# The second layer norm of a fused cross-attention block, moved from ScalarE and GpSimd to VectorE

## The chip, the cores and the metric

The kernel runs on one core of a Trainium2 chip. The metric is the device time of one execution in microseconds. The profile is of one execution, taken by the hardware profiler; its times count from its first instruction. The core has five engines that work side by side, each through its own list of instructions: TensorE (PE; its weight loads are PEld), VectorE (DVE), ScalarE (ACT), GpSimd (POOL), and SyncE (SP), which here only issues DMAs.

## The reference

Everything is float32. For 128 sequences of 128 tokens with 256 features:

```python
q = (query @ Wq + bq).reshape(b, s, 16, 16).transpose(0, 2, 1, 3)
k = (key @ Wk + bk)...            # key and values are ctx_1024
v = (values @ Wv + bv)...
scores = einsum('bhqd,bhkd->bhqk', q, k) / 4
scores = where(j < i, scores, -1e30)
attn = softmax(scores); attn[:, :, 0, :] = 0
attn_out = (attn @ v) @ Wo + bo
x = layer_norm(query + attn_out, ln1_g, ln1_b)
ffn = relu(x @ W1 + b1) @ W2 + b2          # 256 -> 1024 -> 256
out = layer_norm(x + ffn, ln2_g, ln2_b)
```

where `layer_norm(x, g, b) = (x - mu) * rsqrt(var + 1e-5) * g + b` over the 256 features. The change concerns the last line.

## The kernel before

The 128 sequences are worked in 64 pairs; a tile such as `t2` holds one pair as 128 tokens x 2 x 256. The work is software-pipelined by hand: in step p the kernel does the scores and the softmax of pair p, the attention product of pair p-2, the hidden layer of pair p-3, the second matrix of the feed-forward net of pair p-4, and the second layer norm of pair p-5. The schedule is manual: the order of the calls in the source is the order in which each engine gets its instructions, and semaphores only make an engine wait. For pairs 9 to 60 the order is one table of names with lags (lines 1493 to 1513), looked up in `ops` (lines 1359 to 1492); the steps before and after are written out call by call (lines 1567 to 2333 and 2336 to 2915).

What the steps below touch, in the order of one step:

- `scores_both` (L486) writes the scores of a pair into PSUM banks 0 to 3 (second half of the queries) and 6, 7, 4, 5 (first half). `mask` (L511) on VectorE reads the latter; its first call of a step is the one of bank 4 (`low2`). The query products of the next pair (`Query.run`, L351) write bank 4 again, so they come after that mask.
- The softmax runs on ScalarE (L997). `reciprocal` (L566) on VectorE, `sums` (L557) on GpSimd and `turn` (L574, a transpose of 32x32 blocks on VectorE) follow, three times a step. `bring` (L608) moves the transposed blocks by DMA on SP's queue, in which the DMAs of the first norm (`leave_x1` L256, `fetch_x1` L262) stand as well.
- The hidden layer is made of seven products (Strassen's scheme, L1156), which VectorE adds up in `hT` (L1175 to L1187); ScalarE applies the relu in place (L1190), GpSimd forms the sums `hS` for the next stage (L1023 to L1029).
- The second matrix is seven products as well (S1 to S7, L1064); VectorE adds them into `t2` (L1088). S5 is `py<-wt,hS`.
- `Joint` (L1301) collects the statistics of two norms at once: bn_stats (L1313) and bn_aggr (L1318) on VectorE give mean and variance `mv`; `both_shifts` (L720) on GpSimd gives `sd`, the variance plus eps to the power -0.5, and `nb`, minus mean times `sd` (L717, L718, L723, L724).
- `norm2` (L783) then scales and shifts `t2` in place on ScalarE, one half of the pair at a time (`n2a`, `n2b`, L787). `finish` (L791) multiplies by `g2_r` and adds `be2_r` on GpSimd, over the whole pair at once (`fin1` L794, `fin2` L796). `g2_r` and `be2_r` are the two vectors of 256, repeated on all 128 partitions of SBUF. `store` (L815) sends `t2` out on SP's queue two steps later.
- GpSimd's other work of a step: `add_bo` (L274), the residual's scale and shift (L761, L765), the combinations for the seven products of the queries (L320 to L326) and of the hidden layer (L1110 to L1116).

In the table, `n2b` stands before `rcp0`, which is followed by the last sum into `t2` (`add5`) and the hidden adds; `n2a` stands after `Hadd3` and before `turn2`; `fin1` stands after `turn2`; `fin2`, with lag 2, stands among the `hS` sums two steps later.

Pairs 0, 1, 58 and 59 call `norm2` and `finish` directly, 60 to 62 use `norm2_apart` and `finish_apart`, and the last pair ends in `last_scale` (L1553) and `last_shift` (L1559), which are scalar_tensor_tensor instructions on VectorE with one operand in PSUM. Only one early pair normalizes on VectorE (L749, tensor_scalar on an SBUF tile, twice).

Of the kernel before, what the change touches and what calls it, by code (L numbers as in the profile page):

```python
# [11 lines left out]
ALU = mybir.AluOpType  # L12
# [8 lines left out]
def tile_cross_attention_block(  # L21
# [22 lines left out]
    nc = tc.nc  # L44
# [30 lines left out]
    states = {}  # L75
# [45 lines left out]
    def row(v, name, at=None):  # L121
        t = const.tile([P, v.shape[1]], F32, tag=name, name=name) if at is None else early[:, at : at + v.shape[1]]
        nc.sync.dma_start(t, v.to_broadcast([P, v.shape[1]]))
        return t
# [40 lines left out]
    g2_r = row(ln2_g, "g2_r")  # L165
    be2_r = row(ln2_b, "be2_r")
# [49 lines left out]
    def at_bank(i, name):  # L216
        return psum.tile([P, 512], F32, tag=f"b{i}", name=name)
# [519 lines left out]
    def norm1(p, parts=range(2)):  # L737

        st = states[p]
        x1 = st["x1"] = st["t1"]  # L740
        t1, mv, sd = x1, st["mv", 1], st["sd", 1]
        for s in parts:
            if p != 1:

                nc.scalar.activation(
                    x1[:, s], t1[:, s], AF.Identity, bias=st["nb", 1][:, s], scale=sd[:, s]
                )
                continue
            nc.vector.tensor_scalar(  # L749
                x1[:, s], t1[:, s], mv[:, s, 0:1], sd[:, s], ALU.subtract, ALU.mult  # L750
            )

    def residual1(p, engine=nc.gpsimd, parts=range(2)):

        st = states[p]
        if 0 in parts:
            if p < NP - 2:
                st["t2"] = ffn.tile([P, 2, D], F32, tag="t2", name=f"t2_{p}", bufs=4)
            else:
                st["t2"] = proj.tile([P, 2, D], F32, tag="xb", name=f"t2_{p}")  # L760
            engine.tensor_tensor(  # L761
                st["t2"], st["x1"], g1_r[:, None, :].to_broadcast([P, 2, D]), ALU.mult
            )
        if 1 in parts:
            engine.tensor_tensor(  # L765
                st["t2"], st["t2"], be1b_r[:, None, :].to_broadcast([P, 2, D]), ALU.add
            )
# [15 lines left out]
    def norm2(p, parts=range(2)):  # L783
        st = states[p]
        t2, sd, nb = st["t2"], st["sd", 2], st["nb", 2]
        for s in parts:
            nc.scalar.activation(  # L787
                t2[:, s], t2[:, s], AF.Identity, bias=nb[:, s], scale=sd[:, s]
            )

    def finish(p, parts=range(2)):  # L791
        t2 = states[p]["t2"]
        if 0 in parts:
            nc.gpsimd.tensor_tensor(t2, t2, g2_r[:, None, :].to_broadcast([P, 2, D]), ALU.mult)  # L794
        if 1 in parts:
            nc.gpsimd.tensor_tensor(t2, t2, be2_r[:, None, :].to_broadcast([P, 2, D]), ALU.add)  # L796

    def norm2_apart(p, at, parts=range(2)):

        st = states[p]  # L800
        t2, sd, nb = st["t2"], st["sd", 2], st["nb", 2]
        ps = once("pb", p, lambda: at_bank(at, f"pb_{p}").rearrange("p (s d) -> p s d", s=2))
        for s in parts:
            nc.scalar.activation(
                ps[:, s], t2[:, s], AF.Identity, bias=nb[:, s], scale=sd[:, s]
            )
# [8 lines left out]
    def store(p):  # L815
        nc.sync.dma_start(
            out[2 * p : 2 * p + 2].rearrange("b p d -> p b d"), states.pop(p)["t2"]
        )
# [212 lines left out]
    def once(kind, p, make):  # L1031
        st = states[p]
        if kind not in st:
            st[kind] = make()
        return st[kind]
# [180 lines left out]
    for which, first in (("c", c_first[:, 0:2]), ("x", tokens_of[0][:, 0:2])):  # L1216
        st = states[0]
# [113 lines left out]
    def second7(p):  # L1331
        return once("second", p - 4, lambda: Second(p - 4, 6))
# [25 lines left out]
    def step_tables():  # L1358
# [93 lines left out]
            "shifts": lambda p: joint(p).shifts(),  # L1452
            "n1a": lambda p: norm1(p - 2, (0,)),
            "n1b": lambda p: norm1(p - 2, (1,)),
            "n2a": lambda p: norm2(p - 5, (0,)),
            "n2b": lambda p: norm2(p - 5, (1,)),
            "add0": lambda p: second7(p).add(0),
            "add1": lambda p: second7(p).add(1),
            "add2": lambda p: second7(p).add(2),
# [18 lines left out]
            "bo": lambda p: add_bo(p - 1),  # L1478
            "x1g": lambda p: residual1(p - 3, nc.gpsimd, (0,)),
            "x1b": lambda p: residual1(p - 3, nc.gpsimd, (1,)),  # L1480
            "fin1": lambda p: finish(p - 5, (0,)),
            "fin2": lambda p: finish(p - 5, (1,)),
            "store": lambda p: store(p - 5),
            "tbx": lambda p: block_x1(p - 2),
            "x1out": lambda p: leave_x1(p - 2),
# [28 lines left out]
        return ops, order  # L1514

    ops, order = step_tables()

    def steps(first, last):
# [1305 lines left out]
    h62.relu(4)  # L2824
    both_shifts(*j60a)
    norm2_apart(60, 4, (0,))
    w61.add(4)
    norm2_apart(60, 4, (1,))
    w62 = Second(62, banks=(0, 7, 2))
    w62.run(2)  # L2830
# [56 lines left out]
    w62.add(5)  # L2887
    j62a = both_stats((), (62,))
    norm2_apart(61, 3, (1,))
    both_shifts(*j62a)  # L2890
    norm2_apart(61, 3, (0,))
# [59 lines left out]
```

## Time and profile before

| | |
|---|---|
| runs | 1477.25 and 1477.29 us, median 1477.27 us |
| profiled execution: span, first to last instruction | 1476.5 us |
| mean granted TensorE clock | 0.999 of full |
| one step of the steady stretch | 22.45 us |
| pairs normalized through the table's `n2a`, `n2b`, `fin1`, `fin2` | 56 of 64 (2 to 57) |

The profile's page gives the busy time of each engine as a sum and as a share of the span. The timeline has a row for each instruction (equal neighbours are merged, with their count): start and length in us, engine, line, operation, output tile <- input tiles, shapes. A wait in brackets is idle time of that engine just before the row, with the engine, tile and line that ended it. Instructions of one engine overlap a little, so the work that an instruction costs its engine is the distance from its start to the next one's start when nothing is waited for; this is called the hand-over below. Rows of groups give the total busy time and the mean in ns; rows of one line give least, median and greatest duration.

### The profile page before, as it was taken

The page shows a single profiled execution, that of the slowest core. Times are in us where ns is not written, and L with a number is a line of the kernel's source. Part 1 is how long each engine was busy: PE and PEld are TensorE (multiplying, and loading weights), DVE is VectorE, ACT ScalarE, POOL GpSimd, SP SyncE. Part 2 cuts the span into 40 slices and gives each one's busy share as a digit, 9 for nine tenths or more (in the row PEclk, how much of TensorE's full clock was granted, in tenths as well). Part 3 has the DMA queues.
Part 4 walks back from the last instruction along what each step waited for, and adds up shares of the span by engine and source line. Part 5 has one row for each costly group of instructions (what it writes and reads, how often), then busy time and mean ns, then how long its engine had stood idle before and what let it go on. Part 6 is the DMA issues. An engine that isn't in the chain of part 4 may idle for free.

```text
span 1476.5 us, 53972 instructions
## 1 busy us (share of the span) xinstructions
PE 1463.9 (99%) x19696; PEld 1377.8 (93%) x19696; DVE 1315.5 (89%) x2897; ACT 1323.0 (90%) x5279; POOL 1388.2 (94%) x1484
## 2 busy tenths in 40 slices
PE   9999999999999999999999999999999999999998
PEld 7788999999999999999999999999999999999998
DVE  7999899999998998998998999989989999999866
ACT  5758999999999999999999999999999999999863
POOL 7788999999999999999999999999999999999987
PEclk9999999999999999999999999999999999999999
DMA  8465566655656666666556566556565666664451
GB/s 203 96 141 127 133 146 139 147 138 136 156 141 138 141 146 139 148 144 145 138 135 154 139 142 141 144 135 157 141 139 136 146 141 150 136 152 122 116 162 58
DMA packets 417865, 206.22 MB, mean 140 GB/s; under 512 B 282434, under 2 KB 386114, under 8 KB 417602
## 3 DMA queue, kind: packets, MB, share of 16 engines
q1 hardware_dynamic: 416080, 202.49, 58.3%
q8 instruction: 159, 2.61, 0.8%
q14 instruction: 106, 0.85, 0.2%
q10 hardware_dynamic: 1520, 0.27, 0.1%
HBM read 71.84 MB, written 34.87 MB: 72 GB/s over the span
## 4 chain that ended last, share of the span: by engine, by line
PE 95%; DVE 1%; POOL 1%; DMA 1%; SPq 1%; issue 1%; ACT 0%; DVEq 0%; POOLq 0%
PE phs L1156 25%; PE pX L1064 11%; PE po L671 7%; PE pk L281 7%; PE pz L1064 7%; PE py L1064 7%; PE pv L411 7%; PE pq L351 6%; PE pss L502 6%; PE pc L652 4%; PE pc L642 3%; PE ph L917 1%; PE pq L281 1%; PE py L940 1%; SPq L608 1%; POOL sm L557 1%
## 5 line engine op out<-in xcount | busy, mean ns | idle before, releaser
L557 POOL TENSOR_TENSOR sm<-sm,rs 128x1024 f32<-128x1024 f32 x192 | 364.0, 1898 | 2.4 <-DVE rs L566 2.3
L997 ACT ACTIVATE sm<-pss,nmx 128x128 f32<-128x128 f32 x944 | 331.9, 395 | 8.4 <-DVE nmx L980 2.4
L997 ACT ACTIVATE sm<-sm,nmx 128x64 f32<-128x64 f32 x944 | 321.4, 361 | 0.8 <-DVE nmx L987 0.2
L1190 ACT ACTIVATE hT<-hT,b1e_c 128x256 f32<-128x256 f32 x480 | 216.1, 501 | 53.9 <-DVE hT L1181 44.7
L574 DVE STREAM_TRANSPOSE tb<-sm 128x1024 f32<-128x1024 f32 x186 | 227.8, 1226 | 1.5 <-POOL sm L557 1.4
L997 ACT ACTIVATION_READ_ACCUMULATOR sm<-pss,nmx 128x1 f32 x912 | 214.7, 235 | 0.0
L997 ACT ACTIVATION_READ_ACCUMULATOR sm<-sm,nmx 128x1 f32 x912 | 193.8, 212 | 0.0
L1156 PE MATMUL phs<-xS,w1t 128*128 128x128 f32 x1440 | 180.2, 275 | 0.0
L1156 PEld LDWEIGHTS phs<-xS,w1t 128*128 128x128 f32 x1440 | 170.4, 192 | 0.0
L980 DVE TENSOR_REDUCE nmx<-pss 128x4 f32<-128x512 f32 x236 | 160.6, 682 | 1.9
L401 ACT ACTIVATE kT<-pk,bkh,half 128x256 f32<-128x256 f32 x252 | 140.0, 559 | 4.1 <-PE pk L281 4.1
L516 DVE TENSOR_TENSOR sm<-pss,neg 128x256 f32<-128x256 f32 (+1 forms) x276 | 113.8, 436 | 16.5 <-PE pss L502 12.5
L1064 PE MATMUL pX<-wt,hS 128*128 128x128 f32 x960 | 126.8, 275 | 0.0
L1156 PE MATMUL phs<-x1T,w 128*128 128x128 f32 x960 | 126.5, 275 | 0.0
L1156 PEld LDWEIGHTS phs<-x1T,w 128*128 128x128 f32 x960 | 120.7, 192 | 3.0
L671 PE MATMUL po<-wo,cxT 128*128 128x256 f32 x512 | 121.8, 381 | 0.0
L411 PE MATMUL pv<-wv,cT 128*128 128x256 f32 x512 | 120.9, 379 | 0.0
L281 PE MATMUL pk<-cT,wk 128*128 128x256 f32 x504 | 119.5, 380 | 0.0
L1064 PEld LDWEIGHTS pX<-wt,hS 128*128 128x128 f32 x960 | 117.0, 192 | 0.1
L411 PEld LDWEIGHTS pv<-wv,cT 128*128 128x128 f32 x512 | 96.9, 190 | 13.1
L671 PEld LDWEIGHTS po<-wo,cxT 128*128 128x128 f32 x512 | 92.5, 190 | 12.2 <-issue 1.6
L281 PEld LDWEIGHTS pk<-cT,wk 128*128 128x128 f32 x504 | 91.5, 190 | 10.5 <-issue 0.2
(192 smaller groups left out, 4149.3 us busy)
## 6 DMA issues: line engine op xcount, KB each, us to landing
pT<-tb SPq DMA_DIRECT2D x976, 96.0 KB, 2.3
x1t<-tbx SPq DMA_DIRECT2D x252, 64.0 KB, 2.7
x1T<-x1t SPq DMA_DIRECT2D x63, 256.0 KB, 3.4
out_dram<-t SPq DMA_DIRECT2D x63, 256.0 KB, 4.3
xb<-in_x_dram SPq DMA_DIRECT2D x124, 128.0 KB, 3.3
cb<-in_ctx_dram SPq DMA_DIRECT2D x124, 128.0 KB, 3.2
x<-in_x_dram SPq DMA_DIRECT2D x31, 512.0 KB, 5.0
w<-in_L_xattn_W_dram SPq DMA_DIRECT2D x2, 1024.0 KB, 7.8
```

The source lines that it names most:

```text
L281: nc.tensor.matmul(ps[:, m * TP : (m + 1) * TP], w[:, k, m * P : (m + 1) * P], src[:, k, :], start=(k == 0), stop=(k == KC - 1),)
L401: nc.scalar.activation(st["kT"][:, m, e, :], pk[:, m * TP : (m + 1) * TP], AF.Identity, bias=bkh[:, m, e : e + 1], scale=half[:, e : e + 1],)
L411: nc.tensor.matmul(pv[:, s * D : (s + 1) * D], st["cT"][:, k, s * P : (s + 1) * P], wv[:, k, :], start=(k == 0), stop=(k == KC - 1),)
L516: nc.vector.tensor_tensor(probabilities(p, hi)[:, 4 * r : 4 * r + 4, :], st["sps", hi][r][:, : 4 * n].rearrange("p (n j) -> p n j", j=n), ...
L557: nc.gpsimd.tensor_tensor(sm[:, part, :], sm[:, part, :], rs[:, :, None].to_broadcast([P, part.stop - part.start, n]), ALU.mult,)
L574: nc.vector.transpose(st["tb"][:, :, at : at + 256].rearrange("p j (n a) -> p n j a", a=32), probabilities(p, hi).rearrange("p h j -> p (h ...
L671: nc.tensor.matmul(po[:, s * D : (s + 1) * D], cxT[:, k, s, :], wo[:, k, :], start=(k == 0), stop=(k == KC - 1),)
L980: nc.vector.tensor_reduce(maxima(p, 1)[:, 4 * r : 4 * r + 4], st["sps", 1][r].rearrange("p (n j) -> p n j", j=P), AX.X, ALU.max, negate=True,)
L997: nc.scalar.activation(sm[:, h, :], src, AF.Exp, bias=nmx[:, h : h + 1], scale=1.0, **({"accum_out": st["su", hi][:, h : h + 1]} if summed ...
L1064: nc.tensor.matmul(out, left(k), right(k), start=(first and k == 0), stop=(k == K - 1), skip_group_check=True,)
L1156: nc.tensor.matmul(ps[:, i * P : (i + 1) * P].rearrange("p (n a) -> p n a", a=32), left(i), right, start=(i == 0 and which not in self.ONT ...
L1190: nc.scalar.activation(self.hT[:, f], self.hT[:, f], AF.Relu, bias=b1e_c[:, f : f + 1], scale=1.0,)
```

## The change

`n2a` and `n2b` each call a new function `norm2_half`, which issues two scalar_tensor_tensor instructions on VectorE, one for each half of the pair. The first call computes (t2 - mean) * g2, the second (t2 * sd) + be2, both in place in SBUF. `fin1` and `fin2` do nothing. The order of the names is as before, and so are the pairs that don't go through the table.

```diff
+    def norm2_half(p):
+
+        st = states[p]
+        t2, mv, sd = st["t2"], st["mv", 2], st["sd", 2]
+        scaled = st.pop("scaled", False)
+        for s in range(2):
+            if scaled:
+                nc.vector.scalar_tensor_tensor(
+                    t2[:, s], t2[:, s], sd[:, s], be2_r, ALU.mult, ALU.add
+                )
+            else:
+                nc.vector.scalar_tensor_tensor(
+                    t2[:, s], t2[:, s], mv[:, s, 0:1], g2_r, ALU.subtract, ALU.mult
+                )
+        if not scaled:
+            st["scaled"] = True
...
-            "n2a": lambda p: norm2(p - 5, (0,)),
-            "n2b": lambda p: norm2(p - 5, (1,)),
+            "n2a": lambda p: norm2_half(p - 5),
+            "n2b": lambda p: norm2_half(p - 5),
...
-            "fin1": lambda p: finish(p - 5, (0,)),
-            "fin2": lambda p: finish(p - 5, (1,)),
+            "fin1": lambda p: None,
+            "fin2": lambda p: None,
```

Line numbers of the changed kernel are 17 higher from `norm2_apart` on; the new instructions are its L809 (subtract, multiply) and L805 (multiply, add).

On VectorE, step 35 before, from the transpose of the context `cT` to the first mask of the next step (`rs` is the reciprocal, `hT` the hidden adds, `tbx` the first norm's transpose, `tb` the transpose of the softmax, `t_31` a `t2` tile):

```order
L267 STREAM_TRANSPOSE cT_12437<-cb_11482 128x512
L566 RECIPROCAL rs_35_0_12455<-sa_35_12328 128x16
L1088 TENSOR_TENSOR t_31_12184<-t_31_12184,pX_12288 128x256
L1175 TENSOR_TENSOR hT_12345<-hT_12345,phs_7_12423 128x4x128
L1178 TENSOR_TENSOR hT_12345<-hT_12345,phs_5_12430 128x4x128
L1187 TENSOR_TENSOR hT_12345<-hT_12345,phs_2_12459 128x4x128
L1181 TENSOR_TENSOR hT_12345<-hT_12345,phs_4_12465 128x4x128
L882 STREAM_TRANSPOSE tbx_12476<-t_33_12322 128x4x4x32
L1184 TENSOR_TENSOR hT_12345<-hT_12345,phs_5_12430 128x4x128
L574 STREAM_TRANSPOSE tb_12407<-sm_12257 128x8x4x32
L516 TENSOR_TENSOR sm_12620<-pss_36_2_12582,neg 128x256
```

The start of the same stretch in the changed kernel:

```order
L267 STREAM_TRANSPOSE cT_12438<-cb_11484 128x512
L809 SCALAR_TENSOR_TENSOR t_30_11823<-t_30_11823,mv_12376,g_r 128x256 x2
L566 RECIPROCAL rs_35_0_12457<-sa_35_12329 128x16
L1105 TENSOR_TENSOR t_31_12186<-t_31_12186,pX_12290 128x256
L1192 TENSOR_TENSOR hT_12346<-hT_12346,phs_7_12424 128x4x128
```

And its end, from the hidden add of product 4 on:

```order
L1198 TENSOR_TENSOR hT_12346<-hT_12346,phs_4_12467 128x4x128
L899 STREAM_TRANSPOSE tbx_12478<-t_33_12323 128x4x4x32
L1201 TENSOR_TENSOR hT_12346<-hT_12346,phs_5_12431 128x4x128
L805 SCALAR_TENSOR_TENSOR t_30_11823<-t_30_11823,sd_12377,be_r 128x256 x2
L574 STREAM_TRANSPOSE tb_12408<-sm_12259 128x8x4x32
L516 TENSOR_TENSOR sm_12622<-pss_36_2_12584,neg 128x256
```

Two instructions of pair 30 now stand between the `cT` transpose and the reciprocal, and two between the last hidden add and the softmax transpose; nothing else moved.

On GpSimd, one step before, from the third `sums` on:

```order
L557 TENSOR_TENSOR sm_12620<-sm_12620,rs_36_0_12818 128x1024
L274 TENSOR_TENSOR xb_12908<-x_11487,bov_r 128x512
L794 TENSOR_TENSOR t_31_12184<-t_31_12184,g_r 128x512
L761 TENSOR_TENSOR t_33_12912<-t_33_12322,g_r 128x512
L1025 TENSOR_TENSOR hS_13014<-hT_12708 128x512
L765 TENSOR_TENSOR t_33_12912<-t_33_12912,be1b_r 128x512
L1023 TENSOR_TENSOR hS_13014<-hT_12708 128x512
L796 TENSOR_TENSOR t_30_11821<-t_30_11821,be_r 128x512
L1027 TENSOR_TENSOR hS_13014<-hS_13014,hT_12708 128x512
```

And in the changed kernel:

```order
L557 TENSOR_TENSOR sm_12622<-sm_12622,rs_36_0_12820 128x1024
L274 TENSOR_TENSOR xb_12911<-x_11489,bov_r 128x512
L761 TENSOR_TENSOR t_33_12914<-t_33_12323,g_r 128x512
L1042 TENSOR_TENSOR hS_13016<-hT_12709 128x512
L765 TENSOR_TENSOR t_33_12914<-t_33_12914,be1b_r 128x512
L1040 TENSOR_TENSOR hS_13016<-hT_12709 128x512
L1044 TENSOR_TENSOR hS_13016<-hS_13016,hT_12709 128x512
```

The multiplication (L794) and the addition (L796) are gone, and what stood behind each follows directly on what stood ahead of it.

## The prediction

> **What bounds the kernel now.** I read the page first, for the shares of the engines, then one step of the steady stretch with the windows view.
>
> ```profile
> span 1476.5 us, 53972 instructions
> PE 1463.9 (99%) x19696; PEld 1377.8 (93%) x19696; DVE 1315.5 (89%) x2897; ACT 1323.0 (90%) x5279; POOL 1388.2 (94%) x1484
> ```
>
> ```profile
> core 0: us, PE busy (x) PEld busy (x) DVE busy (x) ACT busy (x) POOL busy (x), PEclk, DMA share, GB/s
> 808.91:831.36 22.45, 22.45 (x312) 21.42 (x312) 20.43 (x48) 21.25 (x88) 21.64 (x24) 1.00 0.58 132
> ```
>
> A step takes 22.45 us, and TensorE is busy for all of it at full clock. So TensorE sets the time, and relief for an engine off its path is worth nothing by itself. But nobody has room: VectorE, which receives the new work, idles 22.45 - 20.43 = 2.0 us a step, GpSimd 0.8, ScalarE 1.2. The question is where VectorE's 2.0 us lie and whether TensorE waits if VectorE is late. For that I followed one step in the timeline, VectorE first, then TensorE.
>
> ```profile
> 805.57 0.29 DVE L1088 TENSOR_TENSOR t<-t,py 128x128 f32<-128x128 f32 x1 [0.34 <-PE py L1064]
> ...
> 808.91 0.21 DVE L566 RECIPROCAL rs<-sa 128x16 f32<-128x16 f32 x1
> 809.04 0.36 DVE L1088 TENSOR_TENSOR t<-t,pX 128x256 f32<-128x256 f32 x1
> 809.32 0.68 DVE L1175 TENSOR_TENSOR hT<-hT,phs 128x512 f32<-128x512 f32 x1
> 810.10 0.69 DVE L1178 TENSOR_TENSOR hT<-hT,phs 128x512 f32<-128x512 f32 x1
> 810.93 0.69 DVE L1187 TENSOR_TENSOR hT<-hT,phs 128x512 f32<-128x512 f32 x1
> 811.82 0.69 DVE L1181 TENSOR_TENSOR hT<-hT,phs 128x512 f32<-128x512 f32 x1 [0.21 <-PE phs L1156]
> 812.43 0.71 DVE L882 STREAM_TRANSPOSE tbx<-t 128x512 f32<-128x512 f32 x1
> ...
> 813.63 1.23 DVE L574 STREAM_TRANSPOSE tb<-sm 128x1024 f32<-128x1024 f32 x1
> 814.89 0.76 DVE L516 TENSOR_TENSOR sm<-pss,neg 128x256 f32<-128x256 f32 x2
> ```
>
> ```profile
> 815.61 0.30 PEld L351 LDWEIGHTS pq<-xT,wq 128*128 128x128 f32 x2 [0.17 <-issue]
> ```
>
> ```profile
> 826.92 1.06 PE L1064 MATMUL py<-wt,hS 128*128 128x128 f32 x8
> ```
>
> The step closes on itself through both engines. VectorE adds py (805.57), works to the first place of the new instructions (just ahead of the reciprocal, 808.91), through the hidden adds to the second place (just ahead of the transpose at 813.63), then the transpose and the mask of pss in bank 4 (814.89). That mask frees bank 4, into which the query products of L351 write: TensorE starts them at 815.61 and then runs without a gap to the S5 product of 826.92, whose sum VectorE adds at 805.57 + 22.45 = 828.02. Written as a sum: 3.34 + 4.72 + 1.98 + 12.41 = 22.45.
>
> How much slack is in it? In the first 3.34 us none. In the 4.72 us three adds start late: an add of 128x512 hands over 0.61 us after its start (811.82 to 812.43), and those at 809.32, 810.10 and 810.93 take 0.78, 0.83 and 0.89 to the next, so 0.67 us is waiting and 4.05 work. At L351 TensorE idles 0.17 us. The 12.41 us are TensorE's own work. So **this cycle has 0.84 us of slack**, not 2.0; VectorE's other waits lie inside TensorE's 12.41 us and help nobody on the cycle.
>
> **The change part by part.** It touches 56 pairs (2 to 57).
>
> *Removed.* Two ScalarE and two GpSimd passes per pair:
>
> ```profile
> L787 ACT ACTIVATE t<-t,nb,sd 128x256 f32<-128x256 f32 x120 | 70.4, 590 | 0.0
> L794 POOL TENSOR_TENSOR t<-t,g_r 128x512 f32<-128x512 f32 x60 | 77.5, 1291 | 2.0 <-ACT t L787 2.0
> L796 POOL TENSOR_TENSOR t<-t,be_r 128x512 f32<-128x512 f32 x60 | 76.4, 1274 | 0.0
> ```
>
> That is 2 x 0.59 = 1.2 us of ScalarE and 1.29 + 1.27 = 2.56 us of GpSimd a step, 66 and 144 us in all. TensorE waits for neither in the steady stretch, so I count nothing. Once, in the run-down, the addition does stand in the chain that ended last, for 1.24 us:
>
> ```profile
> 1413.66 1.24 POOL t L796
> ```
>
> Credit: 1 us.
>
> *Added.* Four scalar_tensor_tensor of 128x256 on VectorE. The loop has none of this size; the last pair has, with one operand in PSUM:
>
> ```profile
> 1472.26 0.49 DVE L1553 SCALAR_TENSOR_TENSOR py_last<-py_last,mv_last,g_r 128x256 f32<-128x256 f32 x1
> 1472.66 0.98 DVE L1559 SCALAR_TENSOR_TENSOR t<-py_last,sd_last,be_r 128x256 f32<-128x256 f32 x2
> ```
>
> The first hands over after 0.40 us. That is the lower bound I use: 4 x 0.40 = 1.6 us a step. But these had GpSimd idle beside them and a PSUM operand; the new ones read two tiles (t2 and g2_r or be2_r) from SBUF, while GpSimd reads SBUF nearly all the time. The nearest row is L749, which does this very arithmetic on a 128x256 SBUF tile with two per-partition scalars:
>
> ```profile
> L749 DVE TENSOR_SCALAR t<-t,mv,sd x2: 401/1194/1986, 64.4 to 64.7; 128x256 f32<-128x256 f32 x2
> ```
>
> ```profile
> 64.64 1.90 POOL L533 TENSOR_TENSOR sm<-sm,nmx 128x1024 f32<-128x1024 f32 x1 [1.69 <-DVE nmx L525]
> ```
>
> The same instruction took 401 ns when GpSimd was idle at its start (64.39), and 1986 ns when it began at 64.70, just behind a GpSimd instruction: it ended at 66.69, 0.15 us after GpSimd's (64.64 + 1.90). It was **held until GpSimd's instruction was over**, and GpSimd had taken its turn between the two. Not every SBUF reader is held:
>
> ```profile
> L574 DVE STREAM_TRANSPOSE tb<-sm x186: 1186/1230/1248, 52.0 to 1419.6; 128x1024 f32<-128x1024 f32 x186
> L1313 DVE BATCH_NORM_STATS2 bsb<-t x224: 375/410/421, 132.3 to 1388.2; 128x6 f32<-128x256 f32 x112
> ```
>
> The trace has no VectorE instruction with two SBUF tensors. I take the held price, because L749 is nearest in arithmetic and operands and the new form asks SBUF for more per element than any of the three; two instructions are thin evidence, and both ends stay in the range. [...]
>
> So what is on GpSimd at the two places?
>
> ```profile
> 808.80 0.20 POOL L724 TENSOR_TENSOR nb<-nb,minus 128x4 f32<-128x4 f32 x1
> 808.95 0.73 POOL L320 TENSOR_TENSOR qS<-xT 128x256 f32<-128x256 f32 x1
> 809.76 0.46 POOL L324 TENSOR_TENSOR qS<-xT,qS 128x128 f32<-128x128 f32 x1
> ...
> 810.71 1.90 POOL L557 TENSOR_TENSOR sm<-sm,rs 128x1024 f32<-128x1024 f32 x1
> 812.57 1.30 POOL L274 TENSOR_TENSOR xb<-x,bov_r 128x512 f32<-128x512 f32 x1
> 813.82 1.30 POOL L794 TENSOR_TENSOR t<-t,g_r 128x512 f32<-128x512 f32 x1
> 815.08 1.27 POOL L761 TENSOR_TENSOR t<-t,g_r 128x512 f32<-128x512 f32 x1
> 816.54 1.27 POOL L1025 TENSOR_TENSOR hS<-hT 128x512 f32<-128x512 f32 x1 [0.19 <-ACT hT L1190]
> ```
>
> *First place*, arrival 808.91: the first instruction waits 0.09 for L724, runs 0.40 (to 809.40); L320 goes next, 0.73 (810.13); the second runs to 810.53. Cost 1.62. Behind it on VectorE stand the reciprocal for L557, the pX sum, then the hidden adds that ScalarE's relus and GpSimd's hS wait for.
>
> *Second place*, arrival 810.53 + 4.05 = 814.58. GpSimd starts L324 at 810.53, and with the spacing of the rows L557 at 811.48, L274 at 813.34, and L761 (L794 is gone) at 814.59. One of my two instructions passes before L761 and one after, or both after; either way both are through at L761's 1.27 plus 0.80, about 816.67: L1025 behind it starts 2.9 us after the last hidden add, when they are done. Cost 2.1. Behind it stand the transpose and the masks, and for these TensorE's query products in bank 4.
>
> *Sum.* 1.62 + 2.1 = 3.7 us a step, less 0.84 of slack: 2.86 us. GpSimd loses 1.6 us a step to VectorE and has gained 2.56, so it stays off the path. I count 54 steps of the 56, since the last two pairs lie in the run-down where TensorE waits for other things: 154 us. Against the profiled execution: 1476.5 + 154 - 1 = 1629.5; the median of the runs shown, 1477.27, lies 0.8 over that span, so **1630 us**. The moved transpose also holds back the DMAs behind it on SP, x1T among them:
>
> ```profile
> 818.62 0.45 SPq L262 DMA_DIRECT2D x1T<-x1t  x1
> ```
>
> ```profile
> x1T<-x1t SPq DMA_DIRECT2D x63, 256.0 KB, 3.4
> ```
>
> ```profile
> 823.13 1.05 PE L1156 MATMUL phs<-x1T,w 128*128 128x128 f32 x8
> ```
>
> It lands at 822.0, 1.1 us before TensorE's use; both move by nearly the same (TensorE by 0.84 less), so 0.3 remains: nothing, but it is what is late next.
>
> **The rivals.**
>
> *Held, but a pair of instructions goes through together.* Then the first place costs 0.09 + 0.80 = 0.89; VectorE comes to the second at 813.85 and waits 0.75 for L274 to end, plus 0.80. X = 2.44, less 0.84: 1.6 us a step, 86 us, 1563 us. For it: nothing lies between the two on VectorE. Against: GpSimd's L533 did come between the two L749.
>
> *Not held.* 1.6 - 0.84 = 0.76 us a step, 41 us, 1517 us. For it: L574 and L1313 read SBUF unhindered. Against: L749.
>
> *Not slower: VectorE swallows it.* Unheld instructions that hand over faster than 0.40. The measurement tells about 2% (29.5 us) from no change, that is 0.55 us a step, so the cost must stay under 0.84 + 0.55 = 1.39 us, or 0.35 for each instruction; at 0.21 each nothing is left and the time is 1476 us, the run-down's 1 us gained. For it: the operands come from SBUF, not PSUM, and L1313 of the same size takes 410 ns against 490. Against: that is still more than 0.35, and the four hand-overs would all have to be faster than any row of this size.
>
> *Every instruction waits for a whole neighbour*: 0.73 + 0.46 + 1.27 + 1.27 + 1.6 = 5.3, less 0.84, 4.5 us a step: 1719 us.
>
> [...]
>
> **How the numbers follow.** Forecast 0.62; held pairwise 0.16; not held 0.08; swallowed 0.06; half rate 0.05; whole neighbours 0.03. The range of 1510 to 1675 us leaves out the swallowed case, the whole neighbours and the held half rate. Slower by over 2%: all but the swallowed case, less a little of the unheld one, 0.92; within 2%: 0.07; faster by over 2%: 0.01, as TensorE's busy time alone is 1463.9.
>
> **What would show it.** Right: the new instructions in the loop last well over 0.5 us on average, their ends falling on ends of GpSimd's; the step is about 25.3 us; TensorE idles nearly 3 us a step, most of it before L351 and a little among the hidden products; GpSimd idles some 5 us a step; VectorE is about 95% busy. Wrong: durations all near 0.4 to 0.5 us (not held), or a step of 22.5 us with no gap at L351 (the cycle has more slack than I read), or a step longer than the VectorE rows explain.

## The result, and the profile after

The changed kernel takes 1598.36 us (two runs, 1597.13 and 1599.59) against 1477.27 before: 1.082 times as long, 95% interval 1.079 to 1.085. That is 121 us slower, where 153 were forecast. The page of its profile, first the span, then the busy time of the engines:

```profile
span 1597.9 us, 53948 instructions
...
PE 1490.3 (93%) x19696; PEld 1390.4 (87%) x19696; DVE 1464.0 (92%) x3121; ACT 1274.6 (80%) x5167; POOL 1273.2 (80%) x1372
```

TensorE does the same 19696 products and now idles 7% of the span; ScalarE and GpSimd have lost the work that was moved and idle 20%. No engine is at its limit: the time goes into waits. One steady step in the windows view, from the reciprocal L566 to the next one:

```profile
874.51:898.97 24.46, 22.84 (x312) 21.57 (x311) 22.99 (x52) 20.38 (x87) 19.57 (x22) 1.00 0.54 123
```

The step is 24.46 us instead of 22.45, so 2.01 longer; VectorE's busy time rose from 20.43 to 22.99, GpSimd's fell from 21.64 to 19.57. Now the same stretch of VectorE's timeline as in the prediction, with the two places of the new instructions (L809 the first half, L805 the second):

```profile
873.27 1.31 DVE L809 SCALAR_TENSOR_TENSOR t<-t,mv,g_r 128x256 f32<-128x256 f32 x2
874.51 0.24 DVE L566 RECIPROCAL rs<-sa 128x16 f32<-128x16 f32 x1
...
875.72 0.69 DVE L1195 TENSOR_TENSOR hT<-hT,phs 128x512 f32<-128x512 f32 x1
...
878.72 1.74 DVE L805 SCALAR_TENSOR_TENSOR t<-t,sd,be_r 128x256 f32<-128x256 f32 x2
880.39 1.23 DVE L574 STREAM_TRANSPOSE tb<-sm 128x1024 f32<-128x1024 f32 x1
881.55 1.04 DVE L516 TENSOR_TENSOR sm<-pss,neg 128x256 f32<-128x256 f32 x3
```

Cost of a place is the distance from its first start to the start of what follows: 874.51 - 873.27 = 1.24 us and 880.39 - 878.72 = 1.67 us, 2.91 together. In narrower windows the four stand apart:

```profile
873.27 0.44 DVE L809 SCALAR_TENSOR_TENSOR t<-t,mv,g_r 128x256 f32<-128x256 f32 x1
...
873.63 0.95 DVE L809 SCALAR_TENSOR_TENSOR t<-t,mv,g_r 128x256 f32<-128x256 f32 x1
...
878.72 1.35 DVE L805 SCALAR_TENSOR_TENSOR t<-t,sd,be_r 128x256 f32<-128x256 f32 x1
...
880.00 0.47 DVE L805 SCALAR_TENSOR_TENSOR t<-t,sd,be_r 128x256 f32<-128x256 f32 x1
```

Two of the four run in 0.44 and 0.47 us, two take two to three times as long. GpSimd at the same moments:

```profile
873.16 0.20 POOL L724 TENSOR_TENSOR nb<-nb,minus 128x4 f32<-128x4 f32 x1
873.32 0.98 POOL L320 TENSOR_TENSOR qS<-xT 128x256 f32<-128x256 f32 x1
...
878.50 1.29 POOL L761 TENSOR_TENSOR t<-t,g_r 128x512 f32<-128x512 f32 x1
881.55 1.27 POOL L1042 TENSOR_TENSOR hS<-hT 128x512 f32<-128x512 f32 x1 [1.76 <-ACT hT L1207]
```

The two engines take turns. The first L809 began just ahead of L320 and was not held; L320 then took 0.98 us in place of its 0.73. The second L809 waited for L320 (end 874.30) and ended 0.28 after it. The first L805 came 0.22 us after L761 had begun and ended 0.28 after it (879.79 to 880.07); the second found GpSimd idle, for which 1.76 us of waiting stand at L1042. Over the whole run, least, median and greatest length in ns:

```profile
L809 DVE SCALAR_TENSOR_TENSOR t<-t,mv,g_r x112: 440/810/1709, 159.1 to 1517.7; 128x256 f32<-128x256 f32 x112
```

```profile
L805 DVE SCALAR_TENSOR_TENSOR t<-t,sd,be_r x112: 470/1135/1496, 161.0 to 1519.5; 128x256 f32<-128x256 f32 x112
```

TensorE stands still at two points of a step, at the hidden product behind L1195 and at the query products behind the mask L516:

```profile
875.09 1.15 PE L1173 MATMUL phs<-x1T,w1t 128*128 128x128 f32 x8
876.56 1.13 PE L1173 MATMUL phs<-xS,w 128*128 128x128 f32 x8 [0.32 <-DVE hT L1195]
...
879.10 1.59 PE L502 MATMUL pss<-kT,qT 32*64 32x128 f32 x64
881.99 0.49 PE L351 MATMUL pq<-xT,wq 128*128 128x128 f32 x2 [1.30 <-DVE sm L516]
```

The same products in the trace of before:

```profile
810.73 1.06 PE L1156 MATMUL phs<-x1T,w1t 128*128 128x128 f32 x8
811.62 1.06 PE L1156 MATMUL phs<-xS,w 128*128 128x128 f32 x8
...
814.09 1.59 PE L502 MATMUL pss<-kT,qT 32*64 32x128 f32 x64
815.61 0.49 PE L351 MATMUL pq<-xT,wq 128*128 128x128 f32 x2
```

The ends of TensorE's rows are modelled, so the delay is read from start to start: 875.09 to 876.56 is 1.47 us where it was 0.89, and 879.10 to 881.99 is 2.89 where it was 1.52. The two points cost 0.58 + 1.37 = 1.95 of the 2.01 us.

**Where the 121 us lie.** I followed the 63 transposes into `tbx`, one for each step of VectorE's program, in both traces. The drift of the changed kernel is -0.1 us at step 6, +4.0 at step 7, +9.9 at step 8, +10.6 at step 9, +113.5 at step 60, +117.5 and +120.3 at steps 61 and 62 and +121.2 at the last. So 51 steady steps cost 2.01 us each, 103 us, and the borders of the loop 18. In steps 7 and 8 the order is written out by hand, and there the four new instructions stand back to back. In step 7:

```profile
159.06 2.05 DVE L809 SCALAR_TENSOR_TENSOR t<-t,mv,g_r 128x256 f32<-128x256 f32 x2
161.03 2.34 DVE L805 SCALAR_TENSOR_TENSOR t<-t,sd,be_r 128x256 f32<-128x256 f32 x2
```

4.2 us in all, and hidden adds stand behind them. TensorE waits for these, once in step 7 and once in step 8 (waits from 150 to 200 us):

```profile
PE pc L642 <- DVE hT L1204: 3.7, 1, 3.7
...
PE pss L502 <- DVE hT L1201: 2.8, 1, 2.8
```

### The profile page after: what moved, and what is told of

It reads as the page before. It is cut to its first block, busy times and chain, and to the rows that moved or that the text cites. A ratio compares the mean times of both kernels' runs of the same rounds, so it can differ in the third digit from the quotient of the medians.

```text
span 1597.9 us, 53948 instructions
## 1 busy us (share of the span) xinstructions
PE 1490.3 (93%) x19696; PEld 1390.4 (87%) x19696; DVE 1464.0 (92%) x3121; ACT 1274.6 (80%) x5167; POOL 1273.2 (80%) x1372
## 3 DMA queue, kind: packets, MB, share of 16 engines
q10 hardware_dynamic: 1520, 0.27, 0.1%
## 4 chain that ended last, share of the span: by engine, by line
PE 36%; SPq 21%; DVE 21%; DMA 11%; issue 5%; ACT 4%; POOL 1%; DVEq 1%; ACTq 0%
SPq L608 15%; DMA out_dram<-t 8%; PE pX L1081 4%; PE phs L1173 4%; PE po L671 4%; PE pk L281 4%; PE pz L1081 4%; PE pv L411 4%; SPq L93 4%; ACT hT L1207 3%; PE pq L351 3%; DVE t L805 3%; DVE tb L574 3%; PE py L1081 2%; DVE hT L1198 2%
## 5 line engine op out<-in xcount | busy, mean ns | idle before, releaser
L557 POOL TENSOR_TENSOR sm<-sm,rs 128x1024 f32<-128x1024 f32 x192 | 364.2, 1899 | 127.1 <-PE phs L1173 107.2
L1014 ACT ACTIVATION_READ_ACCUMULATOR sm<-pss,nmx 128x1 f32 x912 | 211.5, 232 | 0.0
L1014 ACT ACTIVATION_READ_ACCUMULATOR sm<-sm,nmx 128x1 f32 x912 | 189.7, 208 | 0.0
L1042 POOL TENSOR_TENSOR hS<-hT 128x512 f32<-128x512 f32 x60 | 76.3, 1271 | 94.4 <-ACT hT L1207 94.4
L401 ACT ACTIVATE kT<-pk,bkh,half 128x256 f32<-128x256 f32 x252 | 134.6, 558 | 4.1 <-PE pk L281 4.1
L351 PE MATMUL pq<-xT,wq 128*128 128x128 f32 x220 | 48.4, 302 | 68.5 <-DVE sm L516 68.5
L516 DVE TENSOR_TENSOR sm<-pss,neg 128x256 f32<-128x256 f32 (+1 forms) x276 | 105.8, 417 | 6.0 <-PE pss L502 3.9
```

What stands on the lines that cost most here:

```text
L401: nc.scalar.activation(st["kT"][:, m, e, :], pk[:, m * TP : (m + 1) * TP], AF.Identity, bias=bkh[:, m, e : e + 1], scale=half[:, e : e + 1],)
L557: nc.gpsimd.tensor_tensor(sm[:, part, :], sm[:, part, :], rs[:, :, None].to_broadcast([P, part.stop - part.start, n]), ALU.mult,)
L1014: nc.scalar.activation(sm[:, h, :], src, AF.Exp, bias=nmx[:, h : h + 1], scale=1.0, **({"accum_out": st["su", hi][:, h : h + 1]} if summed ...
```

## The experiments

In the table the step is the time from the 8th to the 58th of those transposes, over 50 (before: 22.45 us); the ratio is to the kernel before on the same chip. Unless the text says that the whole computation stands, a kernel leaves out what it names.

| kernel | us | ratio, 95% interval | step us |
|---|---|---|---|
| relief alone | 1477.24 | 1.000, 0.999 to 1.001 | 22.45 |
| first place alone | 1516.18 | 1.026, 1.025 to 1.028 | 23.10 |
| fillers at both places | 1500.02 | 1.016, 1.014 to 1.017 | 22.83 |
| GpSimd's order changed | 1571.26 | 1.064, 1.062 to 1.065 | 23.93 |
| second place alone | 1559.29 | 1.055, 1.054 to 1.057 | 23.92 |
| first place with a PSUM operand | 1507.30 | 1.020, 1.019 to 1.022 | 22.95 |
| four tensor_scalar | 1567.42 | 1.061, 1.060 to 1.063 | 23.95 |
| second half later | 1506.47 | 1.020, 1.018 to 1.021 | 22.69 |
| loop alone | 1583.58 | 1.072, 1.069 to 1.074 | 24.47 |
| one at the first place, three later | 1507.84 | 1.021, 1.019 to 1.024 | 22.89 |
| fillers at the first place alone | 1480.33 | 1.002, 1.001 to 1.003 | 22.50 |
| tensor_scalar into PSUM | 1516.76 | 1.026, 1.025 to 1.028 | 23.23 |

**Relief alone.** The second norm of pairs 2 to 57 is left out altogether: neither the old passes nor the new instructions.

```diff
     def norm2_half(p):
-        st = states[p]
...
+        return
```

> Leaves out the second layer norm of pairs 2 to 57 altogether: ScalarE and GpSimd are relieved as in the change, VectorE gets nothing. Theory (TensorE's cycle sets the step; relief off it is worth nothing): 1475 to 1477 us, the step stays 22.45 us. Rival (the relief itself is worth something, and the change's loss is the larger for it): below 1465 us.

1477.24 us, ratio 1.000, step 22.45. ScalarE's and GpSimd's relief is worth nothing; all that follows is the price of the new instructions.

**First place alone.** The second half is left out.

```diff
             if scaled:
-                nc.vector.scalar_tensor_tensor(
-                    t2[:, s], t2[:, s], sd[:, s], be2_r, ALU.mult, ALU.add
-                )
+                pass
```

> Leaves out the second half of the norm (scale by sd, add be2): only the two instructions ahead of the reciprocal remain. Theory (held behind GpSimd, and a cycle with 0.9 us of slack): they cost 1.24 us a step as in the changed kernel, 0.34 over the slack, step 22.8 us, with some 5 us from steps 7 and 8: 1497 to 1503 us. Rival (no slack in the cycle, every us on VectorE counts): step 23.7 us, 1545 us.

The step was 23.10, above the 22.8 expected and below the rival's 23.7. The place cost what it costs in the changed kernel, 877.55 - 876.31 = 1.24 us:

```profile
876.31 1.31 DVE L807 SCALAR_TENSOR_TENSOR t<-t,mv,g_r 128x256 f32<-128x256 f32 x2
877.55 0.24 DVE L566 RECIPROCAL rs<-sa 128x16 f32<-128x16 f32 x1
```

but only 1.24 - 0.65 = 0.59 of it was absorbed. TensorE shows why:

```profile
879.60 1.13 PE L1171 MATMUL phs<-xS,w 128*128 128x128 f32 x8 [0.32 <-DVE hT L1193]
```

From start to start the product comes 1.47 us after the one ahead of it (878.13 to 879.60), 0.58 more than before, so nearly all of the 0.65 is there. The third hidden product accumulates in the bank of the fifth (`ONTO`) and so waits until VectorE's add of the fifth has read it. A late first place reaches TensorE there, ahead of the second place and of L351, and this way is tighter than the one that I had followed.

**Fillers at both places.** The norm is left out; in place of the new instructions stand bn_stats of the same 128x256, which read one SBUF tensor.

```diff
-                nc.vector.scalar_tensor_tensor(...)
+                nc.vector.bn_stats(filler[:, s], t2[:, s])
```

> Leaves out the norm; in place of each of the four instructions stands a bn_stats of the same half tile, which reads one SBUF tensor and is not held in any trace so far. Theory (the hold is the cost): 410 ns each, 4 x 0.37 = 1.48 us a step, 0.58 over the slack, step 23.0 us, 1505 to 1510 us. Rival (any work at these two places costs 2 us a step, whatever its kind): about 1590 us.

The step was 22.83, a little under the 23.0 expected. The two places cost 866.86 - 866.23 = 0.63 (rows below) and 0.65 us, 1.28 together, and 0.38 came through: 0.90 absorbed, as in the changed kernel (2.91 - 2.01).

```profile
866.23 0.71 DVE L806 BATCH_NORM_STATS2 filler<-t 128x6 f32<-128x256 f32 x2
866.86 0.24 DVE L566 RECIPROCAL rs<-sa 128x16 f32<-128x16 f32 x1
```

Two kinds of work at these places cost their length less the same 0.90; the new instructions cost more because they are longer, and GpSimd's rows beside the fillers keep their lengths of before (L320 0.73 and L761 1.28 us, against 0.73 and 1.27).

**GpSimd's order changed.** The whole computation. `sums` (L557) is put ahead of the three query combinations (L320 to L326), and the residual's scale (L761) a step later, so that GpSimd should be idle at both places.

```diff
-    ("qs02", -1), ("qs1", -1), ("qs3", -1), ("sum0", 0), ("bo", 0), ("turn2", 0), ("fin1", 0), ("x1g", 0),
+    ("sum0", 0), ("qs02", -1), ("qs1", -1), ("qs3", -1), ("bo", 0), ("turn2", 0), ("fin1", 0),
...
-    ("x1b", 1),
+    ("x1g", 1), ("x1b", 1),
```

> Complete. The four instructions stand as in the change; on GpSimd alone the order is altered in steps 9 to 60: the third softmax product, which waits for the reciprocal behind the first place, comes ahead of the query combinations, and the residual's scale goes behind the hidden sums' wait, so that GpSimd should be idle at both places. Theory (held behind GpSimd's instruction): 0.45 to 0.5 us each, 1.56 us a step, 0.66 over the slack, step 23.1 us; with the 18 us that steps 7, 8, 61 and 62 lost: 1525 to 1535 us. Rival (two SBUF operands are slow by themselves, 0.8 us on average): step 24.4 us, 1595 us.

Half a miss: 1571.26 us, a step of 23.93.

```profile
882.69 0.84 DVE L809 SCALAR_TENSOR_TENSOR t<-t,mv,g_r 128x256 f32<-128x256 f32 x2
883.45 0.25 DVE L566 RECIPROCAL rs<-sa 128x16 f32<-128x16 f32 x1
...
887.67 1.69 DVE L805 SCALAR_TENSOR_TENSOR t<-t,sd,be_r 128x256 f32<-128x256 f32 x2
889.28 1.23 DVE L574 STREAM_TRANSPOSE tb<-sm 128x1024 f32<-128x1024 f32 x1
```

At the first place the same two instructions now cost 0.76 us, beside a GpSimd that idles 0.99 us ahead of L557. At the second they still cost 1.61, since with L761 gone another neighbour had moved up, which I had overlooked:

```profile
887.40 1.28 POOL L274 TENSOR_TENSOR xb<-x,bov_r 128x512 f32<-128x512 f32 x1
```

0.76 + 1.61 - 0.90 = 1.47, and the step is 1.48 longer. The instructions are not slow by themselves: 440 to 480 ns with GpSimd idle, as long as the one with a PSUM operand in the trace of before (490).

**Second place alone.** The first half is left out.

```diff
-            else:
-                nc.vector.scalar_tensor_tensor(
-                    t2[:, s], t2[:, s], mv[:, s, 0:1], g2_r, ALU.subtract, ALU.mult
-                )
```

> The first half (the subtraction and the multiplication by g2) is left out; the two instructions of the second half stay where they are, behind GpSimd's instruction L761. In the whole change this place takes 1.67 us from VectorE's last instruction before it to the one behind it. If the two places simply add, and the slack of 0.90 us is one for the whole cycle, wherever the delay stands, the step is 22.45 + 1.67 - 0.90 = 23.22 us, and the time about 1477 + 51 x 0.77 + some 5 to 10 at the edges = 1520 to 1528 us. If the second place is dear only because the first has pushed it against L761, the instruction finds GpSimd differently: not held it costs 0.95, the step is 22.50 and the time 1478 to 1486 us.

A miss: a step of 23.92, and 1559 us instead of 1520 to 1528.

```profile
712.45 1.96 DVE L805 SCALAR_TENSOR_TENSOR t<-t,sd,be_r 128x256 f32<-128x256 f32 x2
714.33 1.23 DVE L574 STREAM_TRANSPOSE tb<-sm 128x1024 f32<-128x1024 f32 x1
```

The place costs 1.88 us here, and of that only 1.88 - 1.47 = 0.41 is absorbed. The second place is dear without the first, so the rival falls. But the slack is not one for the cycle: the waits among the hidden adds lie ahead of the second place and are of no use to it, because its delay stops TensorE at L351 and with it the products that those adds wait for. The adds still wait as before:

```profile
710.64 0.69 DVE L1194 TENSOR_TENSOR hT<-hT,phs 128x512 f32<-128x512 f32 x1 [0.21 <-PE phs L1169]
```

```profile
715.92 0.49 PE L351 MATMUL pq<-xT,wq 128*128 128x128 f32 x2 [1.42 <-DVE sm L516]
```

**First place with a PSUM operand.** As the first place alone, but in steps 9 to 60 the second tensor operand is a part of a PSUM bank (128 columns, read twice) and not `g2_r`, so it computes something else; the second half is left out.

```diff
-                    t2[:, s], t2[:, s], mv[:, s, 0:1], g2_r, ALU.subtract, ALU.mult
+                    half_of, half_of, mv[:, s, 0:1],
+                    states[q - 4]["px"][:, None, :].to_broadcast([P, 2, P]), ALU.subtract, ALU.mult
```

> Only the first half runs, at its place, and the second is left out, as in the kernel with place one alone (1516.18 us, a step of 23.10). In steps 9 to 60 its second tensor operand is a bank of PSUM in place of g2 in SBUF (so the numbers computed are others); one SBUF tensor is read in place of two. If what holds it is that VectorE reads two tensors of SBUF while GpSimd runs, it is not held: two instructions of about 0.48 us each, GpSimd's L320 back from 0.98 to 0.73, the place costs about 0.8 in place of 1.24, the slack of 0.59 takes the most of it, a step of 22.65 and 1488 to 1495 us. If any scalar_tensor_tensor is held by a running GpSimd instruction: as with place one alone, 23.10 and 1512 to 1520 us.

```profile
L813 DVE SCALAR_TENSOR_TENSOR t<-t,mv,pX x104: 435/454/473, 205.9 to 1376.3; 128x256 f32<-128x256 f32 x104
```

None of 104 was held, and L320 beside them takes 0.73 again. With one operand moved from SBUF to PSUM the hold is gone. The place costs 0.75, and 27 of the 50 steps are within 0.1 us of 22.60, against 22.45 + 0.75 - 0.59 = 22.61. The time is above the expected range all the same: the other 23, nearly all of them every second step, are 0.1 to 1.6 us longer, 17 us in all. Most of it stands ahead of TensorE's scores (L502, 11.6 us of idle weight loads in 13 rows), where the profile names nothing that was waited for. What stops TensorE there is open.

**Four tensor_scalar.** The four stand where they were, but read one SBUF tensor each; `g2_r` and `be2_r` are left out.

```diff
-                nc.vector.scalar_tensor_tensor(
-                    t2[:, s], t2[:, s], mv[:, s, 0:1], g2_r, ALU.subtract, ALU.mult
-                )
+                nc.vector.tensor_scalar(
+                    t2[:, s], t2[:, s], mv[:, s, 0:1], mv[:, s, 0:1], ALU.subtract, ALU.mult
+                )
```

> All four instructions stand where the change puts them, but as tensor_scalar with two per-partition scalars: one tensor operand of SBUF, none of them reads g2 or be2 (both are left out). If two tensors read from SBUF are what is held, these run at about 0.25 to 0.45 us each whatever GpSimd does: the two places cost about 0.9 each at most, together 1.3 to 1.8, less the slack of 0.90: a step of 22.85 to 23.35 and 1500 to 1530 us. If what counts is that the instruction is on VectorE while GpSimd runs, in any form, they are held as before: 24.4 and 1590 to 1600 us. The row of L749 before (a tensor_scalar of 401 ns in the middle, 1986 ns at most) speaks for some holding in this form too; then the time lies between.

A step of 23.95 lies between the two theories, nearer to the second: they are held. (The 401 ns that the expectation calls the middle of L749's row are the least of its two, and no run shows the 0.25 us: the shortest of the 224 here took 399 ns.) The first of the first place, and GpSimd beside it:

```profile
714.07 0.93 DVE L809 TENSOR_SCALAR t<-t,mv 128x256 f32<-128x256 f32 x1
```

```profile
714.12 0.73 POOL L320 TENSOR_TENSOR qS<-xT 128x256 f32<-128x256 f32 x1
```

It ended 0.15 us after L320, like L749 in the trace of before. And here GpSimd is not made to wait, although VectorE's instruction started first: L320 keeps its 0.73. So two SBUF tensors are not the condition by themselves; a tensor_scalar from SBUF to SBUF is held with one, 0.93 us here.

**Second half later.** The whole computation, with GpSimd's changed order, and `n2a` put a step later behind the third of the low masks.

```diff
-    ("low3", 0), ("q261", 0),
+    ("low3", 0), ("n2a", 1), ("q261", 0),
...
-    ("relu2", 0), ("n2a", 0), ("vz0", 0),
+    ("relu2", 0), ("vz0", 0),
```

> The whole computation. GpSimd's order as in the kernel with its order changed (1571.26 us; first place 0.76, second place held, 1.61), and the second half is moved one step later, behind the third of the low masks, where GpSimd stands idle and VectorE waits for TensorE's products. If the price is only where the instruction stands and what GpSimd does there, the second place costs nothing that the products do not hide, the first costs 0.76 less the 0.59 that place one alone had, a step of 22.6 us, and with some 15 to 18 us at the edges 1498 to 1508 us. If VectorE's busy time itself is the bound (92% in the profile), the same instructions cost the same anywhere: a step of 23.9, 1565 to 1575 us.

1506.47 us and a step of 22.69, as expected. The same arithmetic by the same instructions costs 29 us in place of 121 (94 with GpSimd's order alone). VectorE's busy time is not the bound; the place is. Both instructions are unheld there, 0.87 us for the two (the row below has both; in the kernel with three of the instructions at this place, further down, GpSimd idles 2.03 us here):

```profile
694.86 0.87 DVE L805 SCALAR_TENSOR_TENSOR t<-t,sd,be_r 128x256 f32<-128x256 f32 x2
```

**Loop alone.** The whole computation; the pairs of steps 7, 8, 61 and 62 keep the old passes.

```diff
-            "n2a": lambda p: norm2_half(p - 5),
+            "n2a": lambda p: norm2_half(p - 5) if 8 < p < 61 else norm2(p - 5, (0,)),
...
-            "fin1": lambda p: None,
+            "fin1": lambda p: None if 8 < p < 61 else finish(p - 5, (0,)),
```

> The whole computation: the change in steps 9 to 60 alone; the pairs whose second norm falls into steps 7, 8, 61 and 62 keep the ScalarE and GpSimd passes. In the changed kernel steps 7 and 8 lost 10.6 us up to step 9 and the run-down 7.7 us, against 2.0 us for a step between. If these losses are the new instructions standing back to back while TensorE waits, and the lower clock that follows the wait, they go: a little comes back at each border, some 3 us in all, and the time is 1477 + 52 x 2.01 + 3 = 1582 to 1588 us, with the granted clock back at 1.00 in steps 7 and 8. If the two borders lose the same in any case, because the loop is filled and emptied at a step of 24.46, it is as the changed kernel, 1595 to 1600 us.

1583.58 us, inside the expected range. The drift at the end is 107 us, and 51 steps of 2.02 are 103 of it: of the borders' 18 us some 4 are left, so most of it was the price of the new instructions there and not one of filling and emptying the loop.

**One at the first place, three later.** The whole computation: one of the four at the first place, where it fits into the slack, three behind the low masks; steps 7, 61 and 62 keep the old passes.

```diff
+            "n2a": lambda p: norm2_some(p - 5, ((0, 1), (1, 0), (1, 1))) if 7 < p < 61 else norm2(p - 5, (0,)),
+            "n2b": lambda p: norm2_some(p - 5, ((0, 0),)) if 7 < p < 61 else norm2(p - 5, (1,)),
```

> The whole computation. GpSimd's order as in the kernel with the second half later; of the four instructions one stays at the first place, where 0.40 us fits into the slack of 0.55 to 0.59 measured there, and three stand one step later behind the third of the low masks, where GpSimd is idle and VectorE's waits inside TensorE's 12.4 us add up to 1.29 us (0.79 + 0.34 + 0.16), against 3 x 0.40 = 1.2. Steps 7, 61 and 62 keep the old passes. If only the place and GpSimd decide, the step is back at 22.45 to 22.50 us, TensorE's own, and the time is 1477 to 1486 us: level with before, and not under it, since TensorE is the bound again. If VectorE's waits can't be filled that closely, TensorE waits again for query products or for scores and the step is 22.7 to 23.0, 1490 to 1508 us.

A miss: 22.89, the second theory. The wait has moved once more:

```profile
696.67 1.06 PE L1078 MATMUL pX<-w,hT 128*128 128x128 f32 x8
697.91 1.99 PE L281 MATMUL pk<-cT,wk 128*128 128x256 f32 x8 [0.18 <-ACT sm L1011]
699.74 1.89 PE L411 MATMUL pv<-wv,cT 128*128 128x256 f32 x8
```

```profile
ACT sm L1011 <- DVE nmx L994: 43.3, 46, 1.0
```

Three instructions in a row make the maxima late, ScalarE's exponentials wait 0.9 us a step for these, and TensorE's key products wait for the exponentials. Read from start to start, this is the whole loss: the key products come 1.24 us after the products ahead of them and the next 1.83 us later, where the trace of before has 0.89 (818.78 to 819.67) and 1.73 (819.67 to 821.40). That is 0.45 us, and the step is 0.44 longer. I had counted VectorE's idle time inside TensorE's 12.4 us as free wherever it is used. Its longer waits (0.79 us at 826.23 and 0.34 at 828.01 in the trace of before) lie at the end of that stretch, and the masks and maxima that ScalarE waits for at the start.

**Fillers at the first place alone.** The norm is left out; only the two bn_stats at the first place run.

```diff
-            nc.vector.bn_stats(filler[:, s], t2[:, s])
+            if not scaled: nc.vector.bn_stats(filler[:, s], t2[:, s])
```

> The second norm is left out as a whole; two bn_stats of 128x256 stand at the first place as fillers, none at the second. With fillers at both places the first cost 0.63 us and the step was 22.83. If the first place alone has 0.59 us of slack before TensorE is late, as two scalar_tensor_tensor there suggested (1.24 - 0.65), the step is 22.45 to 22.50 and the time 1477 to 1482 us. If the 0.90 us belong to the cycle as a whole and can all be used at one place, the step is 22.45 as well; if the work at the first place always comes through less the 0.25 us that the sum of the parts suggests, it is 22.7 and 1490 us.

A step of 22.50: 0.62 us of work (676.21 to 676.83) and 0.05 longer. So 0.57 to 0.59 us at the first place are free, by two kinds of instruction.

**tensor_scalar into PSUM.** The norm is left out; at the first place, in steps 9 to 60, two tensor_scalar read the SBUF tensor and write to an unused part of a PSUM bank.

```diff
+                nc.vector.tensor_scalar(
+                    states[q - 4]["px_bank"][:, P : 3 * P], t2[:, s],
+                    mv[:, s, 0:1], mv[:, s, 0:1], ALU.subtract, ALU.mult
+                )
```

> The second norm is left out; at the first place alone, in steps 9 to 60, stand two tensor_scalar of 128x256 that read the same SBUF tensor as in the kernel with four tensor_scalar, but write to an unused part of a bank of PSUM. There, SBUF to SBUF, the two were held by L320 and L324 (0.93 and 0.62 us, the place 1.38). If it is reading one tensor from SBUF that is held, it stays: the place 1.38, less 0.59 of slack, a step of 23.24 and about 1518 us. If it is the form SBUF to SBUF, and not a read, they are free as the bn_stats and the scalar_tensor_tensor with a PSUM operand were: about 0.4 us each, the place 0.65 to 0.75, a step of 22.50 to 22.61 and 1480 to 1487 us (more if stalls at the scores come as in the kernel with the PSUM operand).

The time, 1516.76, is the one that the first theory expected, and the theory is wrong all the same; the row says so:

```profile
L805 DVE TENSOR_SCALAR pX<-t,mv x104: 503/526/550, 202.9 to 1387.8; 128x256 f32<-128x256 f32 x104
```

Not one of 104 was held, where from SBUF to SBUF they ranged from 402 to 1576 ns. They are slower by themselves (526 ns in the middle, where the shortest from SBUF to SBUF took 402), so the place costs 0.99 and the undisturbed step 22.89 (22.45 + 0.99 - 0.59 = 22.85); the rest is the same stall at the scores in every second step (L502, 11.8 us of idle weight loads in 13 rows), again 17 us. Both kernels with the stall let the instructions of the first place use this PSUM bank, and those without it do not; further than that I can't say.

## Why the prediction was right, and where its sizes were off

*TensorE sets the time, and relief elsewhere is worth nothing*: shown by the relief alone, 1.000.

*The cycle through VectorE and TensorE*: right. TensorE's wait before L351 and a smaller one among the hidden products are where the prediction put them (1.30 and 0.32 us). Of the other signs, VectorE is 94% busy and GpSimd idles 4.9 us a step, as named; the step is 24.46 us where 25.3 was named.

*Held by GpSimd*: right, and shown by removal: with GpSimd idle 0.44 to 0.48 us, with an operand in PSUM never over 0.473, and 0.95 to 1.35 beside a running neighbour in the step above. In the middle of all rows the two lines took 810 and 1135 ns, against 454 with the PSUM operand; the tensor_scalar that is held from SBUF to SBUF took 756 and the one into PSUM 526. What in the engines makes one wait for the other no trace shows.

*First place 1.62 us*: too much; it measured 1.24. Of the 0.38, 0.09 is L724, beside which (873.16, 0.20 us) the first L809 ran its 0.44 unheld; 0.19 is the hand-over after a hold, forecast at a full 0.40 and measured at 0.21 (L320's end at 874.30 to L566 at 874.51); 0.04 is the first hand-over (0.36) and 0.06 that L320 was through 0.67 after it.

*Second place 2.1 us*: too much; it measured 1.67. Forecast was to arrive together with L761 and wait for all of it. Counted from the arrival at the first place, VectorE came 0.22 us earlier than forecast (878.72 - 873.27 = 5.45) but L761 0.45 earlier (5.23), so VectorE found it 0.22 under way and 1.07 of it was left (0.20 less), and the hand-over after the hold was 0.21 again (0.19 less).

*Slack 0.84 us*: 0.90 in sum, and right only because both places have work. It is two slacks: 0.59 at the first place, set by the third hidden product that waits for L1195, which the prediction did not follow, and one at the second, where I had read 0.17 from TensorE's idle time at L351: 0.41 when the second place stands alone, and 1.67 - 1.37 = 0.30 behind a busy first place. Work at one place alone can't use the other's.

*54 steps of 2.86 us and 1 us of credit*: the mis-sized terms make it 2.01 in 51 steps, 103 us; against that the four border steps, counted like the others or not at all, cost 18. The forecast had 51 x 2.86 = 146 for the steady steps, 43 too much, and 3 x 2.86 - 1 = 8 for the rest, 10 too little: that leaves the 32 us between 153 and 121, within rounding.

*x1T is what is late next*: no. Its transfer is issued at 884.38 and TensorE uses it at 889.50, so the distance grew from 4.51 to 5.12 us: TensorE was delayed more between the two than the transfer.

*The rivals.* The half rate, which has 0.05 of the forecast's chances, no run shows: unheld, the new instructions took 440 to 480 ns with two SBUF tensors, against 435 to 473 with one of the two in PSUM. Whole neighbours and "not held" fall with the rows above, and so does "swallowed". The prediction's argument against that one was wrong, though: rows of this size do hand over in less than 0.35 us (the two bn_stats at 824.31 in the trace of before in 0.66, those at the first place in 0.63); the new instructions took 0.36 to 0.40 unheld. That a pair goes through together was not decided at the second place, where no second neighbour stood; at the first place the engines alternate.

## What to carry to other kernels

Before moving work to an engine, find the cycle that closes through it and price each insertion point by its own way to the bounding engine: here the same four instructions cost 121 us at two places and 29 at others, while the engines that were relieved gave nothing back. For work that VectorE does from SBUF beside a busy GpSimd, look at what GpSimd runs at that moment: here a scalar_tensor_tensor of 128x256 with two SBUF tensors waited for it (0.95 and 1.35 us, 0.44 to 0.48 unheld) and so did a tensor_scalar from SBUF to SBUF (0.93, 0.40 at least), and one operand in PSUM took the wait away (at most 0.473). Idle time of an engine counts only where it lies on the way to the next waiter, here 0.90 of VectorE's 2.0 us, and a time that fits a theory is no proof until the row that the theory speaks of has been read.

## What was unexpected of the hardware

The granted clock fell at the border. The windows from 160 and 190 us of the changed kernel (the number after the five engines is the clock):

```profile
160.00:170.00 10.00, 6.30 (x169) 5.48 (x168) 7.86 (x15) 3.77 (x10) 5.96 (x6) 0.66 0.33 76
...
190.00:200.00 10.00, 7.21 (x162) 6.03 (x151) 9.30 (x16) 4.89 (x15) 6.90 (x7) 0.83 0.20 46
```

and the same windows with the change in the loop alone:

```profile
160.00:170.00 10.00, 10.00 (x209) 9.22 (x208) 9.33 (x22) 9.19 (x32) 9.35 (x9) 1.00 0.46 109
190.00:200.00 10.00, 10.00 (x76) 9.59 (x75) 8.76 (x22) 9.97 (x56) 9.92 (x10) 1.00 0.68 173
```

After waits of 3.7 and 2.8 us the clock was 0.66 and 0.83 in these windows; without the waits it is 1.00. The waits of 1.3 us in the steady step leave it at 1.00 (874.51 to 898.97).

Which engine waits differed here with the form: scalar_tensor_tensor with two SBUF tensors made GpSimd's L320 wait in its turn, tensor_scalar did not. Over the whole run L320 took 731 ns in the middle before the change, 986 beside the one and 729 beside the other.
